# Group norm of the first and the last sequence by halves, with a logarithm and an exponential in PSUM; second weights held once; a new table of turns

## The chip, the cores and the metric

The kernel runs on one core of one Trainium2 chip. The metric is the device time of one execution in microseconds. Engines are named as in the profile: PE is the tensor engine (PEld its weight loads), DVE the vector engine, ACT the scalar engine, POOL the GpSimd engine, SP the engine that issues most DMAs.

## The reference

One RWKV block over 8 sequences of 256 tokens and 512 channels, float32, 32 heads of 16 channels. In short (E = 512, `_ln` is layer norm, `_token_shift` the row before minus this row):

```python
xn = _ln(x, ln1_w, ln1_b); sx = _token_shift(xn, state[:, i1])
xxx = tanh((xn + sx * maa_x) @ maa_w1)              # five groups of 32
x5 = xn + sx * (maa_stack + xxx @ maa_w2)           # five mixes
w = exp(-exp(time_decay + tanh(x5[1] @ decay_w1) @ decay_w2))
r, k, v, g = x5[3] @ Wr.T, x5[0] @ Wk.T, x5[2] @ Wv.T, silu(x5[4] @ Wg.T)
a = k * v;  out = r . (faaaa * a + s);  s = a + w * s   # per head, token by token
att = (a4 - mean) * rsqrt(var + 1e-5) * gn_w + gn_b     # group norm over 16 channels
x = x + (att * g) @ Wo.T
xn2 = _ln(x, ln2_w, ln2_b);  xk, xr = mixes of xn2 with the row before
x = x + sigmoid(xr @ ffn_Wr.T) * (relu(xk @ ffn_Wk.T) ** 2 @ ffn_Wv.T)
```

## The kernel before, in words

The work of each sequence b falls into three stages, each a function. `inputs_of_scan(b)` does the first layer norm, turns the rows so that channels lie on partitions (`psT1`), makes the five mixes (`psx`, `psm`, tiles `mix`, finished by POOL on L822 or L850), and projects r, k, v and g. The kernel's index q is a half of the 512 channels, m a quarter within it. `scan(b)` runs the recurrence in four blocks of channels. For each block four tiles `vs` are read back from DRAM, into which rows of v were stored (`vo`); DVE, or in a few places POOL (L998), multiplies them with k; DVE scans them along time (L1003); POOL multiplies the result with r (L1006, tiles `st`); and PE gathers the four products with narrow matmuls (L1014). `rest(b)` is group norm, the output projection (`pso`, L440 with Ws and g), the second layer norm, and the feed-forward part (`psfk`, `psfr`, `psfv`). The weights of the four large matrices of `rest` are streamed anew for every sequence.

Nothing is emitted as it is written. Every operation is recorded with its engine, an estimated duration, the buffers that it writes and reads, and for ACT the table and for PE the tile form that it wants. `Plan.order` then lays the operations out: each has a rank, a number from the table `TURNS`, and what is ready is taken by rank. The estimates (`LANDS` and `WAY` for transfers, others written at each operation) decide when a buffer is free and when something is ready, and the instructions of each engine are emitted in the order of their planned start. Each engine works in that order and waits for whatever is late. So a new table and new estimates move the instructions on all engines and both DMA queues.

PE's matmuls come in tile forms: full (128 rows by 128 columns), columns (four narrow matmuls of 32 output columns each), rows32 and rows64 (a part of the contraction rows), and turns through the identity. `Plan.tiles` decides where a projection is cut into narrow pieces, so as to change the form rarely.

Group norm in `rest(b)` before: the scan's output `att` is centred already. ACT squares both halves (L1032), PE averages the squares over each head's 16 channels with `C_MEAN` (L1040), each quarter of the channels onto 32 partitions of one tile `pv`. ACT takes the root (L1045), DVE the reciprocal (L1051). For sequences 0 to 6, ACT then spreads the 32 rows back over 128 partitions with 16 copies (L1073), and POOL multiplies `att` (L1076). For sequence 7, PE spreads them with `C_SEL` (L1059), and DVE multiplies (L1067). ACT applies gn_w and gn_b (L1080); POOL, or DVE for sequence 7, multiplies with g (L1085, L1083).

In `between`, which makes the feed-forward mixes of sequences 0 to 6, ACT writes two scaled copies, t and u, and POOL adds them (L736). The constants, the weights of the mixes (`w2a`, `w2b`) and of the decay (`dw2`) are loaded once at the start by SP's queue, with the large matrices; `w2b` holds the fifth mix's weights four times, once for each group of 32 rows, and `dw2` its weights twice.

## Time and profile before

| | us |
|---|---|
| median of 3 runs | 608.27 (606.26 to 608.39) |
| the profiled execution, first to last instruction | 607.4 |
| PE busy | 596.5 (98%) |
| DVE busy | 539.7 (89%) |
| ACT busy | 519.0 (85%) |
| POOL busy | 511.6 (84%) |

The profile is of one execution; its span, 607.4 us, is 0.9 us below the median of the runs. The record has no separate device time for the profiled execution, so the 0.9 us stand for what lies around the span. Busy times of different engines overlap. A busy PE is not PE at its peak, since the ends of its matmuls are modelled. In rows of groups, "x56" counts instructions, then come the busy time and the mean duration of one in nanoseconds, then the idle time ahead of them and what ended it. PE's rows count two records for each float32 matmul.

### The profile page before, as it was taken

How to read it: one execution, taken by the hardware profiler on the slowest of the kernel's cores; microseconds unless marked ns; L12 is line 12 of the kernel's file. 1: busy time of each engine (PE TensorE's matmuls, PEld its weight loads, DVE VectorE, ACT ScalarE, POOL GpSimd, SP SyncE). 2: the span in 40 equal slices, each digit the busy share in tenths (PEclk: the TensorE clock that was granted, in tenths of full speed). 3: DMA queues.
4: the chain of work that ended last, by engine and by line, in shares of the span. 5: the costliest groups of instructions: out<-in, count | busy, mean ns of one | idle time of the engine just before them, and what ended most of it. 6: DMA issues, size and time to landing. Idle time of an engine off the chain costs nothing.

```text
span 607.4 us, 17029 instructions
## 1 busy us (share of the span) xinstructions
PE 596.5 (98%) x7022; PEld 346.3 (57%) x7022; DVE 539.7 (89%) x492; ACT 519.0 (85%) x1177; POOL 511.6 (84%) x405
## 2 busy tenths in 40 slices
PE   9999998899999999999999999999999999999997
PEld 7575655347634774446654584465744474546464
DVE  5789999799999999998899999999899999995342
ACT  5977879979999999989999999999998899968350
POOL 2989999989979999899989899988889798987020
PEclk9999999799999999999999999999999999999999
DMA  9887695649668789669767987788667878972352
GB/s 316 272 198 209 184 253 170 167 119 284 193 162 227 198 250 244 182 191 253 202 196 214 269 215 213 210 256 216 166 184 195 231 202 216 282 206 74 130 187 77
DMA packets 52638, 124.73 MB, mean 205 GB/s; under 512 B 5841, under 2 KB 11345, under 8 KB 52561
## 3 DMA queue, kind: packets, MB, share of 16 engines
q1 hardware_dynamic: 48048, 119.39, 70.3%
q10 hardware_dynamic: 4512, 4.26, 2.2%
q8 instruction: 55, 0.90, 0.7%
q14 instruction: 23, 0.18, 0.1%
HBM read 115.25 MB, written 8.39 MB: 204 GB/s over the span
## 4 chain that ended last, share of the span: by engine, by line
PE 68%; POOL 14%; ACT 7%; DVE 5%; DMA 3%; issue 2%; SPq 0%; ACTq 0%; DVEq 0%; POOLq 0%
PE ps L440 57%; POOL st L1006 7%; PE ps L1014 7%; POOL mix L822 3%; PE ps L658 2%; POOL vs L998 1%; DVE st L1003 1%; DMA vo<-v 1%; PE ps L862 1%; PE ps L564 1%; DMA x<-in_x 1%; DMA vs<-vo 1%; DVE vs L1001 1%; ACT xh L595 1%; POOL mix L850 1%
## 5 line engine op out<-in xcount | busy, mean ns | idle before, releaser
L1003 DVE TENSOR_TENSOR_SCAN st<-wrep,vs 128x1024 f32<-128x1024 f32 x128 | 287.9, 2273 | 7.1 <-PE ps L1014 3.5
L1006 POOL TENSOR_TENSOR st<-st,r 128x1024 f32<-128x1024 f32 x128 | 254.8, 2008 | 7.4 <-DVE st L1003 6.0
L1001 DVE TENSOR_TENSOR vs<-vs,ps 128x1020 f32<-128x1020 f32 x122 | 142.6, 1199 | 2.0 <-ACT ps L980 1.0
L440 PE MATMUL ps<-Ws,mix 128*32 128x512 f32 (+3 forms) x872 | 115.1, 585 | 0.0
L440 PEld LDWEIGHTS ps<-Ws,mix 128*32 128x32 f32 (+1 forms) x872 | 37.5, 116 | 63.1 <-issue 58.5
L822 POOL TENSOR_TENSOR mix<-mix,xn 128x512 f32<-128x512 f32 x62 | 66.9, 1103 | 4.1 <-DVE mix L806 4.0
L1014 PE MATMUL ps<-st,con 128*32 128x256 f32 x1024 | 63.7, 388 | 2.4 <-POOL st L1006 1.6
L440 PE MATMUL ps<-mix,Wv 128*32 128x256 f32 (+1 forms) x832 | 59.5, 380 | 1.2 <-DVE mix L819 1.0
L440 PE MATMUL ps<-mix,Wk 128*32 128x256 f32 (+1 forms) x856 | 59.8, 380 | 0.0
L440 PE MATMUL ps<-mix,Wr 128*32 128x256 f32 (+1 forms) x712 | 59.2, 380 | 0.0
L440 PE MATMUL ps<-mix,Wg 128*32 128x256 f32 (+1 forms) x544 | 58.1, 380 | 0.1
L440 PE MATMUL ps<-Ws,g 128*32 128x512 f32 (+1 forms) x416 | 58.1, 606 | 0.0
L440 PE MATMUL ps<-mix,Ws 128*32 128x256 f32 (+1 forms) x688 | 57.8, 380 | 0.0
L1014 PEld LDWEIGHTS ps<-st,con 128*32 128x32 f32 x1024 | 33.1, 111 | 30.0 <-issue 9.0
L440 PEld LDWEIGHTS ps<-mix,Wg 128*32 128x32 f32 (+1 forms) x544 | 42.2, 133 | 12.8 <-issue 0.7
L440 PEld LDWEIGHTS ps<-mix,Wv 128*32 128x32 f32 (+1 forms) x832 | 36.6, 116 | 22.4 <-issue 3.0
L440 PEld LDWEIGHTS ps<-mix,Ws 128*32 128x32 f32 (+1 forms) x688 | 39.6, 123 | 16.7 <-issue 1.4
L440 PEld LDWEIGHTS ps<-mix,Wr 128*32 128x32 f32 (+1 forms) x712 | 38.8, 122 | 16.9 <-issue 1.3
L440 PEld LDWEIGHTS ps<-mix,Wk 128*32 128x32 f32 (+1 forms) x856 | 37.0, 115 | 19.8 <-issue 2.2
L804 ACT ACTIVATE ps<-ps,vec 128x256 f32<-128x256 f32 x112 | 45.5, 448 | 2.9 <-PE ps L440 2.0
L1170 ACT ACT_TABLE_LOAD x33 | 42.3, 1283 | 0.6
L736 POOL TENSOR_TENSOR mix<-mix,sx 128x512 f32<-128x512 f32 x28 | 35.5, 1279 | 6.6 <-ACT mix L729 3.7
(143 smaller groups left out, 1000.4 us busy)
## 6 DMA issues: line engine op xcount, KB each, us to landing
vs<-vo SPq DMA_DIRECT2D x128, 512.0 KB, 5.2
Ws<-in_wo SPq DMA_DIRECT2D x16, 512.0 KB, 5.4
Ws<-in_fk SPq DMA_DIRECT2D x16, 512.0 KB, 5.5
Ws<-in_fr SPq DMA_DIRECT2D x16, 512.0 KB, 5.7
Ws<-in_fv SPq DMA_DIRECT2D x16, 512.0 KB, 5.3
x<-in_x SPq DMA_DIRECT2D x9, 512.0 KB, 6.0
vo<-v ACTq DMA_DIRECT2D x15, 256.0 KB, 5.4
out<-o SPq DMA_DIRECT2D x15, 256.0 KB, 3.8
```

The lines of the kernel that those rows point to most:

```text
L440: nc.tensor.matmul(out[i : i + n], lhsT=w[:, i : i + n], rhs=x, start=first, stop=final)
L564: nc.tensor.matmul(ps()[:, 0, :], lhsT=warm[:, 0, 0:P], rhs=warm[:, 0, 0:T], start=True, stop=True)
L595: summed(junk[n], mv, [src[n]], lambda n=n: nc.scalar.activation(junk[n](), src[n](), AF.Copy, accum_out=mv()[:, n, 0:1]), 0)
L658: nc.tensor.transpose(to[:, m, n * P : (n + 1) * P], xh[n]()[:, k * P : (k + 1) * P], idt())
L736: gp(512, t, [t, u], lambda t=t, u=u: nc.gpsimd.tensor_tensor(t(), t(), u(), ALU.add))
L804: act(256, p_, [p_, vec], lambda g=g, q=q, m=m, p_=p_: nc.scalar.activation(p_()[:, m, :], p_()[:, m, :], AF.Identity, bias=col(f"maa_{g}" ...
L822: gp(512, t, [t, xn[q]], lambda q=q, t=t: nc.gpsimd.tensor_tensor(t(), t(), xn[q]()[:, :, 1 : T + 1], ALU.add))
L1001: dve(4 * T, [vs], [vs, kp], lambda m=m, vs=vs, kp=kp: nc.vector.tensor_tensor(vs()[:, :, 1:T], vs()[:, :, 1:T], kp()[:, m : m + 1, 1:T].t ...
L1003: dve(4 * T, [st], [w, vs, first], lambda w=w, vs=vs, st=st: nc.vector.tensor_tensor_scan(st().rearrange("p n t -> p (n t)"), w().rearrang ...
L1006: gp(4 * T, st, [st, r], lambda m=m, st=st, r=r: nc.gpsimd.tensor_tensor(st(), st(), r()[:, m : m + 1, :].to_broadcast([P, 4, T]), ALU.mul ...
L1014: nc.tensor.matmul(pat()[32 * i : 32 * i + 32, 0, :], lhsT=con()[:, s : s + 32], rhs=done[i]()[:, j, :], start=(j == 0), stop=(j == 3),)
L1170: nc.scalar.preload_act_table_set(op.table)
```

## The change

Four things are changed.

- Group norm of sequences 0 and 7. For each half q, eight narrow matmuls with `C_MEAN` put the mean square of every head onto all 128 partitions at once (a tile `pv` of 128 x 512 for each half). ACT takes the logarithm there and then exp(-0.5 x), both in PSUM and from one table, and DVE multiplies `att` with that tile. Root, reciprocal, the 16 copies, POOL's products of sequence 0 and PE's spreading of sequence 7 go. The planner lets an exponential run from the table of the logarithm.
- `w2b` and `dw2` are held once, cut by output channels, and `C_SEL` goes: 448 KB less are loaded at the start.
- The tiles `u` in `between` lie one element further into their buffer.
- The estimates for transfers are new, and so is the whole table `TURNS` (two of its lines stand for it).

```diff
-C_SEL = C_SUM + P
-NCONST = P + C_SEL + 2 * P
+NCONST = P + C_SUM + P
...
-    LANDS = {"vs__": (2.3, 2.45), "s": (0.3, 2.4), "vo_": (0.7, 2.2), "vo__": (0.35, 2.0), "o_": (0.7, 1.2), "x": (1.8, 2.3),
-             "xt": (1.7, 2.0), "xs": (0.7, 0.9), "idt": (0.2, 1.6), "Wfk_": (1.7, 2.7), "Wfr_": (1.7, 2.7),
-             "Wfv_": (1.7, 2.7), "Wo_": (1.7, 2.7)}
-    WAY = 1.4
+    LANDS = {"vs__": 2.33, "s": 0.4, "vo_": 0.85, "vo__": 0.25, "o_": 0.8, "x": 1.55, "xt": 1.5, "xs": 0.9, "idt": 0.2,
+             "Wfk_": 1.69, "Wfr_": 1.62, "Wfv_": 1.7, "Wo_": 1.7, "Wg": 1.6, "Wk": 1.2, "Wr": 1.1, "Wraw": 1.1, "cen": 0.4,
+             "con": 0.5, "dw": 0.5, "mw": 0.7, "mwa": 0.5, "mwb": 0.6, "vec": 0.6}
+    WAY, LANDED = 1.18, 1.15
     TABLES = {"exp": "exp_and_others", "tanh": "exp_and_others", "silu": "silu_and_others", "sig": "sigmoid_and_others",
-              "sqrt": "sqrt_and_others"}
+              "sqrt": "sqrt_and_others", "ln": "natural_log_exp_and_others"}
...
-            op.wire, op.lag = self.LANDS.get("".join(c for c in op.bufs[0].name if not c.isdigit()), (kb / 308, 1.7))
+            op.wire = self.LANDS.get("".join(c for c in op.bufs[0].name if not c.isdigit()), kb / 308)
+            op.lag = self.LANDED
...
     TURNS = """
-        8 72 12 20 41 124 40 135 48 116 79 78 141 119 3 32 84 31 128 181 183 185 11 10 19 39 62 68 36 65 69 37
...
+        2 122 24 50 18 104 49 77 105 42 54 133 87 85 1 29 31 26 142 159 160 163 19 17 43 22 47 51 20 46 68 21
...
                 elif now == "tanh" and want in ("exp", "silu"):
                     mode["ACT"] = now = want
+                elif want == "exp" and now == "ln":
+                    want = now
...
-            u = new("sx", f"u{name}_{q}")
+            u = Buf("sx", f"u{name}_{q}", lambda t: t[:, 1 : 2 * T + 1].rearrange("p (m t) -> p m t", m=2))
...
-                    mul(ps[k]()[:, 0, :], w2b()[rows, k * P : (k + 1) * P], tb()[rows, :], tiles=False)
+                    mul(ps[k]()[:, 0, :], w2b()[rows, :], tb()[rows, :], tiles=False)
...
-        pv, rs = new("ps", f"pv{b}"), sqs[0]
-
-        def mm():
-            for blk in range(NK):
-                rows = slice(32 * blk, 32 * blk + 32)
-                nc.tensor.matmul(
-                    pv()[rows, 0, :], lhsT=con()[:, C_MEAN : C_MEAN + 32], rhs=sqs[blk // 2]()[:, blk % 2 * T : blk % 2 * T + T],
-                    start=True, stop=True)
-
-        pe(0.437, [pv], [con, *sqs], mm, "columns")
-        act(256, rs, [pv, eh], lambda: nc.scalar.activation(
-            rs()[:, 0:T], pv()[:, 0, :], AF.Sqrt, bias=eh()[:, 0:1]), "sqrt", 1)
-        kept = False
-        if kept:
-            dve(256, [pv], [rs], lambda: nc.vector.reciprocal(pv()[:, 0, :], rs()[:, 0:T]), 6.25)
+        split = b == 0 or last
+        if split:
+            pr = []
+            for q, sq in enumerate(sqs):
+                p_ = new("ps", f"pv{b}_{q}")
+
+                def mm(sq=sq, p_=p_):
+                    for m in range(2):
+                        for i in range(0, P, 32):
+                            nc.tensor.matmul(p_()[i : i + 32, m, :], lhsT=con()[:, C_MEAN : C_MEAN + 32],
+                                             rhs=sq()[:, m * T : m * T + T], start=True, stop=True)
+
+                pe(0.864, [p_], [con, sq], mm, "columns")
+                act(512, p_, [p_, eh], lambda p_=p_: nc.scalar.activation(p_(), p_(), AF.Ln, bias=eh()[:, 0:1]), "ln", 1)
+                act(512, p_, [p_], lambda p_=p_: nc.scalar.activation(p_(), p_(), AF.Exp, scale=-0.5), "ln")
+                pr.append(p_)
         else:
+            pv, rs = new("ps", f"pv{b}"), sqs[0]
+
+            def mm():
+                for blk in range(NK):
+                    rows = slice(32 * blk, 32 * blk + 32)
+                    nc.tensor.matmul(
+                        pv()[rows, 0, :], lhsT=con()[:, C_MEAN : C_MEAN + 32], rhs=sqs[blk // 2]()[:, blk % 2 * T : blk % 2 * T + T],
+                        start=True, stop=True)
+
+            pe(0.437, [pv], [con, *sqs], mm, "columns")
+            act(256, rs, [pv, eh], lambda: nc.scalar.activation(
+                rs()[:, 0:T], pv()[:, 0, :], AF.Sqrt, bias=eh()[:, 0:1]), "sqrt", 1)
             dve(256, [rs], [rs], lambda: nc.vector.reciprocal(rs()[:, 0:T], rs()[:, 0:T]), 6.25)
-        if last:
-            pr = [new("ps", f"psr{b}_{q}") for q in range(NQ)]
-
-            def mm():
-                for m in range(2):
-                    for q in range(NQ):
-                        rows, s = slice(64 * q, 64 * q + 64), C_SEL + m * P
-                        nc.tensor.matmul(
-                            pr[q]()[:, m, :], lhsT=con()[rows, s : s + P], rhs=rs()[rows, 0:T], start=True, stop=True)
-
-            pe(0.945, pr, [con, rs], mm, "rows64")
         ys = []
         for q in range(NQ):
             att, g = got["att", q], got["g", q]
-            if last:
+            if split:
                 dve(512, [att], [pr[q], att], lambda att=att, ps=pr[q]: nc.vector.tensor_tensor(att(), ps(), att(), ALU.mult))
             else:
                 rsb = new("rk", f"rsb{b}_{q}") if q else sqs[1]
                 for n in range(2):
                     for i in range(4):
                         rows = slice(32 * i, 32 * i + 32)
-                        act(335 if kept else 376, rsb, [pv if kept else rs], lambda blk=2 * q + n, n=n, rows=rows, rsb=rsb: nc.scalar.copy(
-                            by_block(rsb)[rows, n, :],
-                            (pv()[:, 0, :] if kept else rs()[:, 0:T])[32 * blk : 32 * blk + 32, :]))
+                        act(376, rsb, [rs], lambda blk=2 * q + n, n=n, rows=rows, rsb=rsb: nc.scalar.copy(
+                            by_block(rsb)[rows, n, :], rs()[32 * blk : 32 * blk + 32, 0:T]))
...
-    load(con, consts[:, P:NCONST], 224)
+    load(con, consts[:, P:NCONST], 96)
     load(vec, vecs, 64)
     load(w1, maa_w1.rearrange("(k p) j -> p k j", p=P), 384)
-    load(w2a, maa_w2[0:4].rearrange("g j e -> (g j) e"), 256)
-    load(w2b, maa_w2[4:].rearrange("g j e -> (g j) e"), 256)
+    load(w2a, maa_w2, 256)
+    load(w2b, maa_w2_last, 64)
     load(dw1, decay_w1.rearrange("(k p) j -> p k j", p=P), 128)
-    load(dw2, decay_w2, 256)
+    load(dw2, decay_w2, 128)
...
-        "maa_w2": np.concatenate([a["maa_w2"], *[a["maa_w2"][4:]] * (3)], axis=0),
+        "maa_w2": a["maa_w2"][:4].reshape(4 * MAA, E),
+        "maa_w2_last": np.concatenate([a["maa_w2"][4][:, k * P : (k + 1) * P] for k in range(NK)], axis=0),
         "decay_w1": a["decay_w1"],
-        "decay_w2": np.concatenate([by_channel(a["decay_w2"].T).T] * 2, axis=0),
+        "decay_w2": np.concatenate(np.split(by_channel(a["decay_w2"].T).T, NQ, axis=1), axis=0),
```

How the new table moves instructions is shown at three places. The first is POOL ahead of the gather of sequence 1's first block. Rows with 128x1024 are the products of scanned tiles with r (L1006 before, L1011 now), `mix` rows finish mixes of sequence 2, and `vs` is the product of a tile with k. Before:

```order
L822 TENSOR_TENSOR mix_119<-mix_119,xn_101 128x512
L822 TENSOR_TENSOR mix_122<-mix_122,xn_102 128x512
L822 TENSOR_TENSOR mix_115<-mix_115,xn_102 128x512
L822 TENSOR_TENSOR mix_111<-mix_111,xn_101 128x512
L998 TENSOR_TENSOR vs_149<-vs_149,k_127 128x4x255
L1006 TENSOR_TENSOR st_156<-st_156,r_128 128x1024
L1006 TENSOR_TENSOR st_159<-st_159,r_128 128x1024
L1076 TENSOR_TENSOR att_141<-att_141,sq_162 128x2x256
L1076 TENSOR_TENSOR att_142<-att_142,rk_153 128x2x256
L1006 TENSOR_TENSOR st_155<-st_155,r_128 128x1024
L1085 TENSOR_TENSOR g_138<-att_141,g_138 128x512
L1085 TENSOR_TENSOR g_137<-att_142,g_137 128x512
```

And now, on the same engine (L827 is L822 of before, L1003 is L998, L1091 is L1085):

```order
L1003 TENSOR_TENSOR vs_149<-vs_149,k_127 128x4x255
L827 TENSOR_TENSOR mix_115<-mix_115,xn_101 128x512
L1011 TENSOR_TENSOR st_156<-st_156,r_128 128x1024
L827 TENSOR_TENSOR mix_122<-mix_122,xn_101 128x512
L827 TENSOR_TENSOR mix_111<-mix_111,xn_102 128x512
L1011 TENSOR_TENSOR st_155<-st_155,r_128 128x1024
L1011 TENSOR_TENSOR st_157<-st_157,r_128 128x1024
L1091 TENSOR_TENSOR g_137<-att_141,g_137 128x512
L1091 TENSOR_TENSOR g_138<-att_142,g_138 128x512
```

The two group norm products are gone, and the product with k stands ahead of three mixes that it followed before.

The second place is PE at the same gather: two pieces of a k projection, the fifth mix of sequence 2 (`tb`, `mw2b`), and the gather's first row, before:

```order
L440 MATMUL ps_175<-mix_122,Wk_76 32x256 x8
L440 MATMUL ps_175<-mix_111,Wk_77 32x256 x8
L440 MATMUL ps_175<-tb_124,mw2b 128x256
L440 MATMUL ps_172<-tb_124,mw2b 128x256
L440 MATMUL ps_174<-tb_124,mw2b 128x256
L440 MATMUL ps_177<-tb_124,mw2b 128x256
L1014 MATMUL ps_175<-st_155,con 32x256
```

Now the gather follows the k projection at once; this is PE from the gather's last row on (L445 is L440 of before, L1019 is L1014), with the output projection of sequence 0 (`Ws`, `g`):

```order
L1019 MATMUL ps_172<-st_155,con 32x256
L445 MATMUL ps_175<-Ws_168,g_137 32x512 x8
L445 MATMUL ps_175<-Ws_169,g_138 32x512 x8
L445 MATMUL ps_173<-Ws_168,g_137 32x512 x8
L445 MATMUL ps_172<-tb_124,mw2b 128x256
L445 MATMUL ps_177<-tb_124,mw2b 128x256
L445 MATMUL ps_175<-tb_124,mw2b 128x256
L445 MATMUL ps_174<-tb_124,mw2b 128x256
L445 MATMUL ps_173<-Ws_169,g_138 32x512 x8
```

The fifth mix moved from ahead of the gather to between the output projections.

The third place is the start of SP's queue. `Ws` are the raw weights of v (two halves) and a small matrix from `consts`, `mw` the first mixing weights, `dw` the first decay weights. Before:

```order
L429 DMA xt_88<-in_x 128x512 x2
L429 DMA Ws_167<-in_wv 128x2x512
L429 DMA Ws_168<-in_consts 128x128
L429 DMA vec<-in_vecs 128x128
L429 DMA Ws_169<-in_wv 128x2x512
L429 DMA mw_66<-in_maa_w 128x4x192
```

Now:

```order
L434 DMA xt_88<-in_x 128x512 x2
L434 DMA Ws_167<-in_wv 128x2x512
L434 DMA mw2a<-in_maa_w 128x512
L434 DMA Ws_168<-in_consts 128x128
L434 DMA vec<-in_vecs 128x128
L434 DMA Wk_77<-in_wk 128x2x512
L434 DMA Ws_169<-in_wv 128x2x512
L434 DMA dw_69<-in_decay_w 128x4x64
L434 DMA mw_66<-in_maa_w 128x4x192
```

Three loads (256, 512 and 128 KB) moved ahead of the first mixing weights. Counted over the whole order, PE changes its tile form 97 times now and 101 times before; ACT has 36 loads of tables now and 34 before; PE has 24 more narrow matmuls for group norm and 4 fewer wide ones for spreading.

More of the change, by code (lines that the diff above doesn't have):

```diff
@@ L364, in tables @@
                 want = "silu" if want == "silu" else "exp"
+            elif want == "exp" and mode == "ln":
+                want = mode
             if want != mode:
@@ L388, in tile_rwkv_block @@
     maa_w2: bass.AP,
+    maa_w2_last: bass.AP,
     decay_w1: bass.AP,
@@ L421, in tile_rwkv_block @@
         "x2": lambda t: t[:, :, 1 : E + 1],
+        "sx": lambda t: t[:, 0 : 2 * T].rearrange("p (m t) -> p m t", m=2),
     }
@@ L452, in tile_rwkv_block @@
     idt, con, vec = const("idt", [P, P]), const("con", [P, NCONST - P]), const("vec", [P, NK, NVEC + 2 * NB])
-    w1, w2a, w2b = const("mw1", [P, NK, 6 * MAA]), const("mw2a", [P, E]), const("mw2b", [P, E])
-    dw1, dw2 = const("dw1", [P, NK, DEC]), const("dw2", [2 * DEC, E])
+    w1, w2a, w2b = const("mw1", [P, NK, 6 * MAA]), const("mw2a", [P, E]), const("mw2b", [P, P])
+    dw1, dw2 = const("dw1", [P, NK, DEC]), const("dw2", [2 * DEC, 2 * P])
     hm = const("hm", [P, NK, 32])
@@ L470, in tile_rwkv_block @@
     pool("xn", 4, [P, 2, T + 1])
-    pool("sx", 4, [P, 2, T])
+    pool("sx", 4, [P, 2 * T + 2])
     pool("mix", 14, [P, 2, T])
@@ L885, in mm @@
                 for q in range(NQ):
-                    rows, k = slice(DEC * q, DEC * q + DEC), 2 * q + m
-                    mul(pw[q]()[:, m, :], dw2()[rows, k * P : (k + 1) * P], hd()[rows, 1, :], tiles=False)
+                    rows = slice(DEC * q, DEC * q + DEC)
+                    mul(pw[q]()[:, m, :], dw2()[rows, m * P : (m + 1) * P], hd()[rows, 1, :], tiles=False)
         pe(0.945, pw, [dw2, hd], mm, "rows64", ws)
@@ L1182, in _constants @@
             con[:, C_SUM + 32 * i + 4 * h + i] = head == h
-            con[32 * i + 4 * h, C_SEL + P * (i % 2) : C_SEL + P * (i % 2 + 1)] = head_v == h
     same = head_v[:, None] == head_v[None, :]
```

267 rows, old and new, of the table TURNS are left out of this document.

## The prediction

> **What bounds the kernel now.** I read the page's sums first, then the busy time by stage, the waits of the tensor engine, and the chain that ended last.
>
> ```profile
> span 607.4 us, 17029 instructions
> PE 596.5 (98%) x7022; PEld 346.3 (57%) x7022; DVE 539.7 (89%) x492; ACT 519.0 (85%) x1177; POOL 511.6 (84%) x405
> ```
>
> PE is the bound over the whole span. The stages say where it is not. The columns are span, then busy time of PE, PEld, DVE, ACT and POOL with counts, the granted clock, the DMA share and GB/s.
>
> ```profile
> 0.00:15.00 15.00, 13.78 (x86) 11.76 (x90) 8.44 (x24) 8.19 (x19) 4.02 (x20) 1.00 0.92 315
> 45.00:105.00 60.00, 57.94 (x1020) 34.52 (x1016) 60.00 (x52) 49.26 (x103) 60.00 (x43) 1.00 0.77 209
> 105.00:120.00 15.00, 12.23 (x190) 6.51 (x184) 10.81 (x11) 14.21 (x33) 15.00 (x10) 0.85 0.58 147
> 120.00:135.00 15.00, 15.00 (x184) 6.12 (x180) 13.74 (x11) 12.24 (x29) 12.73 (x12) 0.93 0.51 132
> 135.00:555.00 420.00, 419.86 (x4990) 240.87 (x4979) 405.38 (x332) 390.46 (x900) 386.28 (x294) 1.00 0.77 214
> ```
>
> From 135 to 555 us PE is busy 419.86 of 420: there only fewer matmuls or fewer changes of form shorten anything. Up to 120 us POOL and DVE are full (60.00 of 60 each), PE has idle time, and right after it the clock falls. A finer cut of the same view:
>
> ```profile
> 95.40:98.80 3.40, 2.37 (x46) 1.30 (x41) 3.40 (x5) 3.32 (x7) 3.40 (x4) 1.00 0.87 211
> ...
> 112.00:115.40 3.40, 1.49 (x24) 0.52 (x16) 2.73 (x2) 3.35 (x8) 3.40 (x4) 1.00 0.91 234
> 115.40:118.80 3.40, 2.54 (x24) 1.18 (x28) 1.40 (x4) 3.37 (x10) 3.40 (x4) 0.50 1.01 240
> 118.80:122.20 3.40, 3.40 (x24) 0.99 (x20) 2.23 (x2) 3.30 (x7) 3.40 (x3) 0.50 0.91 228
> ```
>
> In 112.0 to 115.4 PE was busy 1.49 of 3.40 us, and then ran at half clock for 6.8 us, which is 3.4 us of full-speed work lost. With 2.37 of 3.40, in 95.4 to 98.8, nothing followed. PE's waits in the span, longest in total first:
>
> ```profile
> PE ps L1014 <- POOL st L1006: 1.6, 1, 1.6
> PE ps L440 <- ACT k L901: 1.2, 1, 1.2
> PE ps L862 <- POOL mix L822: 1.0, 1, 1.0
> ```
>
> The chain that ended last (start, us, what) names what holds that place up:
>
> ```profile
> 38.70 2.37 POOL vs L998
> ...
> 108.18 3.98 POOL st L1006 x2
> 112.16 2.09 POOL att L1076 x2
> 114.25 1.97 POOL st L1006
> 116.26 3.64 PE ps L1014 x32
> 119.90 10.89 PE ps L440 x104
> 130.78 1.86 PE ps L1014 x32
> ...
> 174.71 1.73 PE ps L1014 x32
> ...
> 381.55 0.48 PE ps L1040 x8
> ...
> 559.81 3.43 PE ps L440 x32
> 563.24 1.06 PE ps L1059 x8
> ```
>
> POOL's window between the first of these rows and the gather at 116.26 is a block without a hole, and two products of `rest(0)` follow it:
>
> ```profile
> 38.70:116.20 77.50, 77.50 (x53) 0.99 0.74 197
> 116.14 2.16 POOL L1085 TENSOR_TENSOR g<-att,g 128x512 f32<-128x512 f32 x2
> ```
>
> So the gather of sequence 1's first block (L1014) stands at 116.26 because POOL has 77.5 us of work in a row ahead of it, and 2.09 of them are the two group norm products L1076 of sequence 0, which the change takes off POOL.
>
> **The change part by part.** Prices, by groups (busy, mean ns of one, idle before):
>
> ```profile
> L1073 ACT COPY rk<-sq 32x256 f32<-32x256 f32 x56 | 22.5, 402 | 1.3 <-ACT v L901 0.4
> L1051 DVE RECIPROCAL sq<-sq 128x256 f32<-128x256 f32 x8 | 13.9, 1736 | 2.5 <-ACT sq L1045 2.5
> L1067 DVE TENSOR_TENSOR att<-ps,att 128x512 f32<-128x512 f32 x2 | 1.3, 685 | 1.9 <-PE ps L1059 1.9
> L1100 ACT ACTIVATE mix<-ps 128x512 f32<-128x512 f32 x16 | 9.3, 588 | 7.2 <-PE ps L440 7.2
> L1080 ACT ACTIVATE att<-att,vec 128x256 f32<-128x256 f32 x32 | 17.3, 592 | 3.5 <-DVE att L1067 3.3 <-POOL att L1076 0.2
> L1170 ACT ACT_TABLE_LOAD x33 | 42.3, 1283 | 0.6
> L736 POOL TENSOR_TENSOR mix<-mix,sx 128x512 f32<-128x512 f32 x28 | 35.5, 1279 | 6.6 <-ACT mix L729 3.7 <-ACT sx L734 2.8
> L822 POOL TENSOR_TENSOR mix<-mix,xn 128x512 f32<-128x512 f32 x62 | 66.9, 1103 | 4.1 <-DVE mix L806 4.0
> L440 PE MATMUL ps<-tb,mw2b 32*128 32x256 f32 x64 | 5.7, 426 | 1.2 <-ACT k L901 1.2
> ```
>
> *Norm of sequence 0, engine by engine.* ACT loses 16 copies (16 x 0.402 = 6.4 us) and a root, and gains four 512-wide passes over PSUM. No row has a logarithm; the nearest, L1100, is as wide and reads PSUM too, so 4 x 0.59 = 2.4, and 4.7 if it takes twice as long; either is less than what goes. DVE loses a reciprocal (1.74) and gains two products (2 x 0.69). POOL loses 2.09. PE now has 16 narrow matmuls for the norm, 32 records, for which the chain has 1.73 (L1014 x32), where it had 8 records, 0.48: +1.25. All but POOL's part lies beside POOL's full block; on the path stands -2.1.
>
> *What this moves at the gather.* With POOL still full from 38.70, the last product of that block is done at 116.2 - 2.1 = 114.1, and the two L1085 products end at 116.3. The output projection of sequence 0 (L440, Ws and g) waits for both; before, it started at 119.90, since the gather in front of it ran at half clock (3.64 against 1.73). Gain: 119.9 - 116.3 = 3.6. Is PE there in time? POOL's order now has the long L998 product ahead of the last three mixes and only two block products behind them, so the last mix comes at 114.1 - 3.98 = 110.1. The k projection that needs it (two groups of 32 records, 3.5) ends at 113.6, half a microsecond before the gather can start. PE's idle time is then spread in pieces of about 1, 0.5 and 0.5 us ahead of the r projection, the k projection and the gather, instead of 1.2 and 1.6 within one 3.4 us window, and the 1.25 us of new matmuls lie in it.
>
> *The clock.* If no 3.4 us window falls below half, 2.3 us at half clock after 119.9 go too: -1.15. [...]
>
> *Moved matmul.* The last mix of sequence 2 (tb, mw2b) leaves the place before the gather, where it filled a wait, and now stands between the output projections: 5.7 / 8 = +0.7 on the path.
>
> *Norm of sequence 7.* PE: 1.73 against 0.48 + 1.06 = 1.54 (L1040 and L1059, whose spreading matmul goes), so +0.2 on a PE that is full. The chain of the second half is two passes (2 x 0.59), three other ACT passes queued behind them (3 x 0.59, DVE's product of 0.69 beside them), four L1080 (4 x 0.59) and a product (0.69): 6.0 us. Its cover is the receptance projection, whose four halves are twice the 3.43 row, 6.9 us. So it is hidden with 0.9 to spare; if that cover is gone, the output projection of sequence 7 waits for the excess alone.
>
> *Tables.* Two loads more, 36 against 34: 2 x 1.28 = 2.6 us of an ACT that is busy 390 of 420 and waits elsewhere; 0 on the path. [...]
>
> *Offset of the `u` tiles.* POOL's sum of two tiles at an equal offset takes 1279 ns, with one moved by an element 1103: 28 x 0.18 = 4.9 us less on POOL, all after 135 us where PE is full: 0.
>
> *Loads.* 448 KB less, and a new order: the rows on the first mixing weights (mw) are
>
> ```profile
> 3.56 0.47 SPq L429 DMA_DIRECT2D mw<-in_maa_w  x1
> mw<-in_maa_w SPq DMA_DIRECT2D x1, 384.0 KB, 6.4
> 11.20 1.96 PE L440 MATMUL ps<-mix,mw 128*128 128x256 f32 x8
> ```
>
> They land at 10.0 and are used at 11.2. Now 896 KB more go first (mw2a, half of Wk, dw1); at 315 GB/s 2.9 us, so they land at 12.9 and the first mixing starts 1.7 us late. All loads end 448 KB / 315 = 1.4 us sooner, and the first stored rows of v queue behind the loads. What counts is POOL's start at 38.70, which hangs on those DMAs: between -1.4 and +1.7; I take +0.2, nearer the middle since both act.
>
> *New turns elsewhere.* PE changes its tile form 97 times instead of 101. A gather with a change takes 1.86, without 1.73: 4 x 0.13 = -0.5. The bounds are 0 and a new wait, which the rivals hold.
>
> *Sum:* -3.6 - 1.15 + 0.7 + 0.2 + 0.2 - 0.5 = -4.1 us. The profiled span goes from 607.4 to 603.3. The runs have a median of 608.27, 0.9 above the span, so the time becomes 604.2 us.
>
> **The rivals.**
> 1. *The clock still halves.* POOL still ends PE's waits, so idle time stays before the gather. It decides if PE is busy for less than some share of a 3.4 us window, which lies between 1.49 and 2.37 us by the two rows above. For it: my pieces of 0.5, 0.5 and the wait for L1085 fall close together. Against: 1.0 alone did not bring it. Price +3.4: 607.6 us.
> 2. *The late start goes through.* POOL starts 1.7 instead of 0.2 late because the mixing weights are late: +1.5, 605.7 us; and with more of PE idle in front, the clock may fall as well: 609.1.
> 3. *Slower: DVE waits for the logarithm.* DVE works in order and is full (60.00 of 60). Its new product of `att` with PSUM waits, if they are not done, for PE's group, a table load and two passes (0.87 + 1.28 + 1.18 = 3.3 us), with scans queued behind it, and each late scan is a late POOL. At one half this is 3.3, at both 6.7; from 4.1 on the gain is gone, PE waits before the gather again and the clock falls as now: 608.3 - 4.1 + 6.7 + 3.4 = 614.3 us. Against: ACT has 10.7 us of idle time in 45 to 105, and the products stand several scans behind their groups.
> 4. *All waits vanish.* 1.6 + 1.2 + 1.0 and 3.4 of clock: 608.3 - 7.2 = 601.1.
>
> **How the numbers follow.** The forecast has 0.54, rival 1 0.20, rival 2 0.10, rival 3 0.11, rival 4 0.05. The forecast's own range is 602.5 to 605.7. For 8 in 10 I reach to 600.8 on one side (rival 4) and to 609.2 on the other (rivals 1 and 2, leaving rival 3 out). A measurement tells apart about 0.5%, 3.0 us: faster means under 605.2. The forecast lies there but for a small part, and rival 4: 0.54 for faster. Rivals 1 and 2 and the rest of the forecast are within: 0.34. Slower: rival 3 and a clock that falls twice, 0.12.
>
> **What would show it.** Right: no L1076 products for sequence 0; the gather after them starts at about 114 and the output projection at about 116.3; granted clock 1.00 in 105 to 135; loads of tables 2 more; L736's heir at about 1.1 us; POOL still full from about 39 to 116. Wrong: a half-clock stretch anywhere past 20 us (rival 1); POOL's first L998 after 40 (rival 2); DVE idle ahead of the new product with a wait on ACT (rival 3); a PE wait on ACT or DVE near 565 (cover of sequence 7 gone).

## The result, and the profile after

The changed kernel takes 609.8 us (median of 12 runs in two sets of six; 607.84 to 611.37), the kernel before 607.0 and 606.5 beside the two sets, and 606.2 to 607.0 beside all the runs below. The ratio is 1.0052 with an interval of 1.0029 to 1.0075 in the first set and 1.0052 (1.0032 to 1.0071) in the second: half a per cent slower, where 604.2 us, 0.7% under its base of 608.3, was forecast. Three of the 110 executions of the kernel before that ran beside the experiments took 691, 1040 and 2196 us, and the ratios leave them out.

The page of the changed kernel, the lines that answer to those of before:

```profile
span 606.1 us, 17579 instructions
PE 595.6 (98%) x7302; PEld 341.6 (56%) x7302; DVE 541.0 (89%) x492; ACT 520.2 (86%) x1169; POOL 504.9 (83%) x403
```

Its busy time by stage (span, then PE, PEld, DVE, ACT, POOL with counts, granted clock, DMA share, GB/s):

```profile
0.00:15.00 15.00, 12.30 (x74) 10.20 (x78) 7.60 (x20) 7.50 (x15) 3.04 (x17) 1.00 0.90 319
...
105.00:120.00 15.00, 14.93 (x246) 7.67 (x239) 14.31 (x10) 12.72 (x28) 15.00 (x12) 1.00 0.64 163
120.00:135.00 15.00, 14.58 (x190) 7.88 (x183) 14.73 (x16) 13.24 (x34) 13.69 (x11) 1.00 0.91 252
135.00:555.00 420.00, 418.91 (x5127) 236.03 (x5129) 402.71 (x329) 391.81 (x897) 379.86 (x293) 1.00 0.76 208
```

At the gather everything stands where it was forecast: PE is busy 14.93 of 15 between 105 and 120, the clock is 1.00 throughout, and POOL's block begins at 39.15 and ends with the two products at 116.65, which is 114.54 + 2.11 (forecast: 116.3), as the chain says:

```profile
39.15 2.36 POOL vs L1003
...
110.58 3.96 POOL st L1011 x2
114.54 2.11 POOL g L1091 x2
```

But PE starts worse (12.30 of the first 15 us, before 13.78) and is no longer full from 135 to 555 (418.91, before 419.86). The prices of the groups came out as forecast: the logarithm 0.66 us, the exponential 0.58, POOL's sum of two tiles 1.09, and two loads of tables more:

```profile
L1053 ACT ACTIVATE ps<-ps,eh 128x512 f32<-128x512 f32 x4 | 2.6, 662 | 0.2 <-PE ps L1049 0.2
L1054 ACT ACTIVATE ps<-ps 128x512 f32<-128x512 f32 x4 | 2.3, 582 | 0.1
L741 POOL TENSOR_TENSOR mix<-mix,sx 128x512 f32<-128x512 f32 x28 | 30.3, 1091 | 5.0 <-ACT mix L734 4.8 <-ACT xn L673 0.2
L1176 ACT ACT_TABLE_LOAD x35 | 44.9, 1283 | 0.6
```

In all six runs of the first set, time less span is 1.7 to 1.8 us, and the spans go from 606.1 to 609.4. The forecast had taken 0.9 us for time less span, from the kernel before, so the first run below is of that kernel.

### The profile page after: what moved, and what is told of

It is laid out like the page before. It is cut to its first block, busy times and chain, and to the rows that moved or that the text cites. A ratio compares the mean times of both kernels' runs of the same rounds, so it can differ in the third digit from the quotient of the medians.

```text
span 606.1 us, 17579 instructions
## 1 busy us (share of the span) xinstructions
PE 595.6 (98%) x7302; PEld 341.6 (56%) x7302; DVE 541.0 (89%) x492; ACT 520.2 (86%) x1169; POOL 504.9 (83%) x403
## 4 chain that ended last, share of the span: by engine, by line
PE 61%; POOL 13%; DVE 9%; DMA 7%; ACT 6%; issue 3%; SPq 0%; ACTq 0%; DVEq 0%
PE ps L445 51%; PE ps L1019 6%; POOL st L1011 6%; DVE st L1008 4%; DMA vs<-vo 3%; POOL mix L827 3%; PE ps L663 2%; POOL vs L1003 2%; DVE vs L1006 1%; DMA vo<-v 1%; PE ps L867 1%; DMA x<-in_x 1%; DVE mix L811 1%; ACT att L968 1%; DMA mw2a<-in_maa_w 1%
## 5 line engine op out<-in xcount | busy, mean ns | idle before, releaser
L1011 POOL TENSOR_TENSOR st<-st,r 128x1024 f32<-128x1024 f32 x128 | 254.6, 2002 | 13.8 <-DVE st L1008 12.9
L1006 DVE TENSOR_TENSOR vs<-vs,ps 128x1020 f32<-128x1020 f32 x122 | 142.6, 1200 | 0.7 <-ACT ps L985 0.6
L445 PE MATMUL ps<-Ws,mix 128*32 128x512 f32 (+3 forms) x920 | 115.1, 586 | 0.1
L445 PEld LDWEIGHTS ps<-Ws,mix 128*32 128x32 f32 (+1 forms) x920 | 36.6, 115 | 64.0 <-issue 57.4
L827 POOL TENSOR_TENSOR mix<-mix,xn 128x512 f32<-128x512 f32 x62 | 66.7, 1092 | 6.5 <-DVE mix L811 5.6
L1019 PE MATMUL ps<-st,con 128*32 128x256 f32 x1024 | 62.9, 381 | 1.1 <-ACT g L936 0.9
L445 PE MATMUL ps<-mix,Wv 128*32 128x256 f32 (+1 forms) x856 | 60.2, 380 | 0.3 <-DVE mix L824 0.3
L445 PE MATMUL ps<-mix,Wr 128*32 128x256 f32 (+1 forms) x688 | 59.8, 380 | 0.0
L445 PE MATMUL ps<-mix,Wk 128*32 128x256 f32 (+1 forms) x880 | 59.3, 379 | 0.0
L445 PE MATMUL ps<-mix,Ws 128*32 128x256 f32 (+1 forms) x760 | 57.9, 379 | 0.7 <-DVE mix L716 0.7
L445 PE MATMUL ps<-mix,Wg 128*32 128x256 f32 (+1 forms) x592 | 58.2, 380 | 0.0
L445 PE MATMUL ps<-Ws,g 128*32 128x512 f32 (+1 forms) x464 | 57.4, 593 | 0.0
L445 PEld LDWEIGHTS ps<-mix,Wg 128*32 128x32 f32 (+1 forms) x592 | 42.1, 129 | 13.4 <-issue 1.0
L445 PEld LDWEIGHTS ps<-mix,Ws 128*32 128x32 f32 (+1 forms) x760 | 38.3, 119 | 19.5 <-issue 2.6
L445 PEld LDWEIGHTS ps<-mix,Wv 128*32 128x32 f32 (+1 forms) x856 | 36.8, 115 | 21.5 <-issue 2.0
L445 PEld LDWEIGHTS ps<-mix,Wr 128*32 128x32 f32 (+1 forms) x688 | 39.4, 123 | 16.3 <-issue 1.3
L1019 PEld LDWEIGHTS ps<-st,con 128*32 128x32 f32 x1024 | 32.5, 110 | 28.0 <-issue 7.1
L445 PEld LDWEIGHTS ps<-mix,Wk 128*32 128x32 f32 (+1 forms) x880 | 36.7, 114 | 20.5 <-issue 1.8
L999 ACT ACTIVATE vs<-s,cm 128x4 f32<-128x4 f32 x128 | 35.6, 296 | 5.5 <-DMA vs<-vo 4.6
```

Of the source, the lines that this page charges most:

```text
L445: nc.tensor.matmul(out[i : i + n], lhsT=w[:, i : i + n], rhs=x, start=first, stop=final)
L827: gp(512, t, [t, xn[q]], lambda q=q, t=t: nc.gpsimd.tensor_tensor(t(), t(), xn[q]()[:, :, 1 : T + 1], ALU.add))
L999: plan.add("ACT", 0.19336, [first], [s0, cm, landed], lambda i=i, blk=blk, vs=vs: nc.scalar.activation(vs()[:, :, 0:1], s0()[:, blk, 4 * i ...
L1006: dve(4 * T, [vs], [vs, kp], lambda m=m, vs=vs, kp=kp: nc.vector.tensor_tensor(vs()[:, :, 1:T], vs()[:, :, 1:T], kp()[:, m : m + 1, 1:T].t ...
L1011: gp(4 * T, st, [st, r], lambda m=m, st=st, r=r: nc.gpsimd.tensor_tensor(st(), st(), r()[:, m : m + 1, :].to_broadcast([P, 4, T]), ALU.mul ...
L1019: nc.tensor.matmul(pat()[32 * i : 32 * i + 32, 0, :], lhsT=con()[:, s : s + 32], rhs=done[i]()[:, j, :], start=(j == 0), stop=(j == 3),)
```

## The experiments

Two terms return below: e5 is the change without its new order, and "lost time" is the time that passed less the matmuls' own length. For that length one full matmul of 256 columns, or four narrow ones side by side, counts the same in every row: 1.2% less than 0.432 us, the most frequent distance of two such matmuls in the traces of the kernel before and of the changed one. The choice moves the levels and hardly the differences: counted with 0.432 us, the first profiles of these two have 6.6 us less each by 600 us, and still lie 3.2 apart. Medians of the kernel before differ by up to 0.8 us between sets of runs, so a difference of that size between two sets shows little by itself.

**The base, and the parts of the change one by one (e1 to e4).**

e1, the kernel before, unchanged.

> The kernel before, unchanged, to see each run's span beside its time. Time less span: about 0.9 us in every run, as in the one profile of before (608.3 less 607.4), where the changed kernel has 1.77 in all six. Theory L (landings: the new turns leave less room for DMAs to land late): the spans lie within 605.3 to 607.5, closer together than the 606.1 to 609.4 of the changed kernel, and what spread there is goes with the granted clock. Rival O (the new order is simply longer, whatever the DMAs do): says nothing else here.

606.76 us. Time less span is 1.7 to 1.8 us in each of its 12 runs, so what lies around the span did not change, and the execution profiled at first, with its span of 607.4, took about 609.2 us: 2 to 3 us more than the usual run. The spans go from 602.9 to 606.2. In 7 of the 12 runs the mean granted clock is 0.996 or 0.997; in the other 5 it is 1.000 and four of those are the four shortest. The first profile had 0.994. Theory L's range is missed (the spans spread by 3.3 us, as the first six of the changed kernel do), but part of the spread does go with the clock. The profile of e1 fell on the shortest run. Its view of the cores, then its chain of waits:

```profile
core 0: 602.9 us, clock 1.000
```

```profile
37.16 2.34 POOL vs L998
...
114.68 1.93 PE ps L1014 x32
116.61 9.66 PE ps L440 x104
```

This is the kernel before, with nothing changed, and its output projection (L440) starts at 116.61, not at 119.90: 3.3 of the 3.6 us that the forecast put down to the removed products lie between two executions of the same kernel. POOL's block starts 1.5 us sooner here. The profile names ACT and DVE as what PE waits for ahead of the gather, and no POOL product (PE's waits of e1, longest first, then the last step of the chain):

```profile
PE ps L1014 <- DVE cm L941: 1.5, 1, 1.5
PE ps L440 <- ACT k L901: 1.3, 1, 1.3
```

```profile
114.53 0.14 DVE cm L941
114.67 0.01 issue
114.68 1.93 PE ps L1014 x32
```

POOL's last product ahead of the gather (L1006) ends at 114.61 in the same trace, 0.06 us before DVE. So two paths of about the same length end here, and a shorter one through POOL need not bring the gather forward.

e2, the changed kernel, unchanged.

> The changed kernel, unchanged, for a second profile. Time less span 1.77 again. Spans again 606 to 609.5 at a clock of 1.00. Theory L: a profile of a longer run differs from the first (606.1) by a few stalls of one to two us at places where a loaded vs tile is awaited, past 135 us, with the same busy time of PE. Rival O: a longer run has its extra time spread evenly, in no single wait, or in busy time of PE.

609.78 us, spans 606.1 to 609.6, time less span 1.7 to 1.8. The second profile has a span of 608.2. From 135 to 555 PE is busy 1.1 us less than in the first:

```profile
135.00:555.00 420.00, 417.79 (x5089) 235.43 (x5091) 403.40 (x330) 390.14 (x896) 377.54 (x291) 1.00 0.76 208
```

The largest of its waits in total is on ACT for `ta` (2.0 us in three waits); e10 takes up the longest, of 1.1. The lost time between the two profiles is in pieces of 0.2 to 1 us in many places: that decides for neither theory.

e3, before with the second weights held once:

```diff
-const("mw2b", [P, E])                      load(w2b, maa_w2[4:]..., 256)
+const("mw2b", [P, P])                      load(w2b, maa_w2_last, 64)
-const("dw2", [2 * DEC, E])                 load(dw2, decay_w2, 256)
+const("dw2", [2 * DEC, 2 * P])             load(dw2, decay_w2, 128)
```

> Before with the second weights held once (mw2b 64 KB from an input of its own, dw2 128 KB) and nothing else; 320 KB less to load. Theory W (the additional input tensor makes the time around the span): time less span 1.7. Rival N (the norm, with its table set and its 280 more matmuls, makes it): 0.9. Span: the loads end 320 KB / 315 GB/s = 1.0 us sooner, so POOL's block starts up to 1.0 earlier: span 0 to 1.0 us under that of the kernel before; 0 if POOL's start hangs on something else.

606.88 us, 1.0010 of before (0.9996 to 1.0024), time less span 1.7 to 1.8: no effect of the weights is to be seen, and POOL's block starts at 37.1, where e1 has 37.2. Both theories on the time around the span fall: there was nothing to explain.

e4, before with the new norm. The diff is that of the change's `rest`; in the table of turns only the 32 entries of the norm's own operations are new.

> Before with the new norm of sequences 0 and 7 alone: old weights, old offset of u, old turns and cost tables, with new places only for the norm's own instructions. Theory N: time less span 1.7; theory W: 0.9. Span, theory L and my prediction's steps: the two POOL products go (-2.1), the clock no longer halves (-3.4 and -1.15), two groups more of PE stand in front of the gather (+1.25): 603 to 605 against 606 to 607.4. Rival O (the norm's work on PE eats the gain): 606.5 to 608.

605.72 us, 0.9994 (0.9982 to 1.0007). Spans 603.4 to 605.9, and the clock fell in 1 run of 12 instead of 7. Where it didn't fall the median span is 603.9, against 603.6 in the five such runs of e1: at full clock the norm gains nothing, and what it brings is a clock that falls less often (here and in e5 in 5 of 24 runs; in the kernel before beside all the runs in 63 of 107). The spans lie where theory L had them, but the 3 us between them and the usual run of before are not there: the medians are 603.9 and 605.0.

**All but the order (e5).** The changed kernel's code, with the cost tables and the turns of before:

```diff
-    LANDS = {"vs__": 2.33, "s": 0.4, ...}      WAY, LANDED = 1.18, 1.15
+    LANDS = {"vs__": (2.3, 2.45), ...}         WAY = 1.4
-    TURNS (new)
+    TURNS (before, with the norm's entries of e4)
```

> The changed kernel's computation, weights, tables and offset of u, but with the turns and the cost tables of before (the norm's own instructions placed as in e4). Theory T (the loss is in the new turns): 605.7 us, as e4 without the new weights and offset. Rival U (the new weights or the offset of u cost something): 607 or more.

605.39 us, 0.9996 (0.9980 to 1.0011). Theory T holds: norm, weights and offset together are not slower than before, and the new order, turns and cost tables together, costs 4.4 us. The clock fell in 4 of the 12 runs. This run also shows what the two products were worth at the gather in the old order (e5's chain):

```profile
115.38 0.14 DVE cm L944
115.52 0.01 issue
115.53 1.93 PE ps L1017 x32
```

The products are gone, POOL's last product ahead of the gather ends at 114.24, and the gather still starts at 115.53, later than in e1, because DVE is what PE waits for. DVE now makes the two products itself (0.68 and 0.69 us), and waits 0.6 us for ACT's exponential ahead of the second. In e4's profile it is the same: POOL ends at 115.01, the gather starts at 115.98, on DVE.

**Cutting the order in two (e6 to e8, e9, e11).** Each operation got its turn of before or its new turn, by the time at which its order starts it.

> The changed kernel with the turns of before for all work that the old order starts before 45 us (the loads among it), the new turns after that. The lost time of PE in the profiles (time less the matmuls' own length) says that the new order loses 1.3 us more than before up to 30 us, 0 to 0.6 from there to 90, wins 2.1 between 90 and 120, and loses again 0.8 from 120 to 150, 0.2 to 1.0 to 180, 1.1 to 1.5 from 360 to 390, and about 1 at the end. Theory P (the loss is these pieces, each from its own place in the order): 609.8 less 1.3 to 2: 607.8 to 608.5. Rival D (delays of landing DMAs anywhere, which an earlier start doesn't mend): 609.5.

609.7 us, 1.0074 (1.0045 to 1.0103), rival D's number, and the clock fell in 3 of the 6 runs. The 1.3 us at the start are saved in the profile (lost time 7.35 by 30 us), but behind the cut PE waits for `g`, which the new order needs sooner than the old one makes it, so the run decides nothing.

```profile
PE ps L859 <- ACT g L928: 2.3, 1, 2.3
```

> As e6, with the turns of before for all work up to 140 us and the new turns after. Theory P: the start's 1.3 to 2 and the 0.8 after the gather are saved, the gain of 2.1 at the gather is given up: 609 to 610. If the new turns after 140 us cost nothing: 605.7.

611.33 us, 1.0088 (1.0062 to 1.0114).

> As e6, with the turns of before for all work up to 345 us and the new turns after. Theory P: what stays is the piece from 360 to 390 and the end, 2 to 2.5 us over e5: about 608. If the late part of the new order costs nothing: 605.7; a time above e7's: the cut itself disturbs.

610.1 us, 1.0071 (1.0050 to 1.0092). Both were slower than their theories had it; the clock fell in 4 of 6 runs of e7 and in 1 of 6 of e8. Ahead of these cuts the old order, under the new cost tables, lost 1.5 and 2.5 us more by 135 than in e5, in profiles where the clock fell after the gather. So the sums can't be read; the part behind the cut can, in e8: 11.4 us lost from 345 to 600, 8.25 in e5. Theory P's times fall in all three runs; its late part is borne out by that loss alone.

> The reverse of e8: the changed kernel with the new turns up to 345 us and the turns of before after that. Theory L (most of the loss is late in the order: 345 to 390 us and the end; PE loses 11.4 us in e8 from 345 to 600 and 8.25 in e5): 609.8 less 2.5 to 3.2: 606.6 to 607.3, with spans as close together as those of e5. Rival S (the loss lies at the start and around the gather, and e8 was slow by its cut alone): 609 to 610.

607.79 us, 1.0014 (1.0001 to 1.0027), 2.0 less than the changed kernel, and the 12 spans lie within 605.5 and 606.9. Nearly half of the loss is behind 345 us, and so is much of the spread. Theory L holds in its direction; the gain is less than its 2.5 to 3.2.

> As e6 with the cut at 80 us, where the two orders have done nearly the same work, so that the cut disturbs less: old turns for the loads and all work up to 80, new ones after. Theory: PE's lost time by 75 us 8.9 and not 10.5 to 11.2, POOL's block starts at 37.2 to 38.7, the gather stays at about 113 to 115 at full clock: 1.3 to 1.6 under the changed kernel, 608.2 to 608.5. Rival (what is won at the start is taken back by POOL's block, which then waits elsewhere): 609.8.

607.33 us, 1.0005 (0.9989 to 1.0021): 2.5 less, more than expected. Cut at a place where both orders have done the same work, the start is a part of the loss as large as the late one; the intervals of e9 and e11 overlap, so which is larger is not decided.

Lost time of PE up to a time, worked out from the matmuls of each profile (us; the first row is the execution profiled at first; the span of each stands ahead; the first profile of the changed kernel is its shortest run, e2's is near its median of 608.0, and e11's is the longest of its 12, which have a median of 605.6):

```
                 span     30     75    105    135    345    405    570    600
before          607.4   7.35   9.45  13.42  20.16  27.15  29.57  35.07  36.03
before, e1      602.9   7.35   8.81  11.71  15.88  22.87  25.34  30.37  32.19
all but order, e5 603.3 7.35   8.86  12.14  15.45  22.23  24.61  29.09  30.48
changed         606.1   8.63  10.51  13.74  15.66  22.87  26.31  31.12  32.83
changed, e2     608.2   8.63  11.15  14.16  16.30  24.38  28.23  32.93  34.75
old turns <80, e11 608.4 7.56  9.23  12.67  14.81  22.02  26.53  33.36  35.18
e12             602.6   7.35   8.97  12.14  14.38  21.59  24.06  28.67  30.48
```

**What in the late part (e10).** In both profiles of the changed kernel PE waits for `ta` at about 373 us, for 0.7 and 1.1 us. SP's timeline in the first, and the `vs` load among the DMA issues of that stretch (KB each, us from issue to landing):

```profile
360.72 0.37 SPq L434 DMA_DIRECT2D xt<-in_x  x1
361.18 0.42 SPq L434 DMA_DIRECT2D Ws<-in_fr  x1
362.10 0.52 SPq L434 DMA_DIRECT2D vs<-vo  x1
362.71 0.54 SPq L434 DMA_DIRECT2D Ws<-in_fv  x1
```

```profile
vs<-vo SPq DMA_DIRECT2D x1, 512.0 KB, 8.6
```

The chain goes from that load to ACT's sequencer, which has a store of v's rows next in its queue (L981), then over `ta` to PE:

```profile
359.87 2.21 DVE st L1008
...
362.10 7.64 DMA vs<-vo
...
370.79 0.37 ACTq L981
...
372.69 0.28 ACT ta L786
```

```profile
ACT ps L848 <- issue: 1.7, 1, 1.7
```

The `vs` load is issued when its buffer comes free (DVE's row ends at 362.08); in the order of before (e5) `xt` and both weights come behind it, and now 1 MB goes ahead of it. e10 puts these two loads behind it again:

```diff
 SP's queue at 361 us
-xt  Wfr3_1  vs5_1_0  Wfv3_0  s
+vs5_1_0  xt  Wfr3_1  Wfv3_0  s
```

> The changed kernel with two places changed in the queue of loads: at about 361 us the load of xt for sequence 7 and the second load of Wfr of sequence 3 go behind the vs load that is issued 1 us later and landed 8.6 us after its issue, where 4.3 to 6 are usual. Theory B (that vs load is late because 1 MB goes ahead of it, ACT waits for it with its work on ta queued behind, and PE for ta): the vs load lands in 5 to 6 us, ACT's wait at 370 and PE's wait for ta of 0.7 to 1.1 go, PE's lost time from 360 to 375 falls from 1.75 to 0.7: 1.0 us under the changed kernel, 608.8. Rival (the load is late for its buffer, which comes free at 362.1 in either order): no difference.

608.35 us, 1.0025 (1.0010 to 1.0040), 1.4 less than the changed kernel. The load now lands in 5.6 us, and ACT's wait is gone:

```profile
vs<-vo SPq DMA_DIRECT2D x1, 512.0 KB, 5.6
```

```profile
ACT ps L847 <- issue: 0.2, 1, 0.2
```

(L847 is L848 of the changed kernel.) PE's lost time from 360 to 375 is 1.11 and not 1.75 (2.18 in e2). Theory B holds; the 1.4 us are more than the 0.6 to 1.1 that this stretch lost less.

**What at the start (e13 to e15).** The chain of the changed kernel into POOL's block:

```profile
25.34 8.92 DMA vo<-v
34.26 0.02 issue
34.27 4.80 DMA vs<-vo
39.08 0.07 issue
39.15 2.36 POOL vs L1003
```

The second store of v's rows (`vo<-v`) takes 8.9 us, behind four `vs` loads. In e1 three go ahead of it (DMA issues of that stretch):

```profile
vs<-vo SPq DMA_DIRECT2D x3, 512.0 KB, 7.1
vo<-v ACTq DMA_DIRECT2D x1, 128.0 KB, 6.7
```

e13 moves the fourth behind the first load of the second half, and with it the scan work on that tile on ACT, DVE and POOL:

```diff
 SP's queue from 23 us on
-vs0_0_2  vs0_0_3  vs0_0_1  vs0_0_0  vs0_1_3  vs0_1_0
+vs0_0_2  vs0_0_3  vs0_0_1  vs0_1_3  vs0_0_0  vs0_1_0
```

> The changed kernel with one load moved at the start: the fourth vs load (the last of the first half of sequence 0) goes behind the second store of v's rows and the first vs load of the second half, as before; the scan work on that tile goes a few places later on ACT, DVE and POOL. Theory F (four loads of 512 KB ahead of the second store of v's rows, where before had three, make POOL's block start late): that store lands at 32.5 to 33.5 and not at 34.3 to 35.3, POOL's block starts at 37.2 to 38.2 and not at 38.6 to 39.7, the time falls by 512 KB / 315 GB/s = 1.7: 608.2. Rival W (what counts is the late landing of mw and PE's late first mixing, 1.3 us, which this doesn't mend): no change, 609.8.

608.75 us (7 runs), 1.0033 (1.0017 to 1.0050): 1.0 of the 1.7 expected, in an interval that overlaps that of the changed kernel. The store takes 7.8 us and lands at 33.4, as theory F has it, and POOL starts without a wait for a DMA, but at 38.8:

```profile
L1003 POOL TENSOR_TENSOR vs<-vs,k x1: 2347/2347/2347, 38.8 to 38.8; 128x1020 f32<-128x1020 f32 x1
```

So the store came as expected and POOL's start did not: 38.8 lies outside theory F's 37.2 to 38.2, and e10, which leaves this load where it was, has 38.6.

> e13 and e10 together: three loads moved in the queue of the changed kernel, nothing else. If both are causes of their own: 609.8 less 1.5 (e10) and 1.7: 606.6, so that two places in SP's queue make up most of the 4.4 us between the changed kernel and e5. If e10's gain was by chance: 608.

607.43 us, 1.0018 (1.0006 to 1.0031). The two gains add (1.4 and 1.0 from 609.8 make 607.4): three loads, moved by one or two places in the queue, and the scan work that goes with one of them, are 2.4 of the 4.4 us. Against e10 alone the fourth load is worth 0.9 here, so its gain was seen twice. How it comes about is not shown: POOL's block starts at 39.2 in this profile, and PE's lost time by 105 us is 13.4 in e13 and 13.8 here, against 13.7 and 14.2 in the changed kernel and 13.4 in e10.

> e14 and one change more in the queue of loads at the start: mw, the first mixing weights, goes ahead of mw2a, half of Wk and dw1 (896 KB), as before. Theory M (my rival 2: the late mixing weights delay all that follows, POOL's block too, and are the second half of the start's loss): mw lands at 9.6 to 10.0 and not at 11.5 to 11.7, PE has lost 7.4 us by 30 us and not 8.6 to 9.2, POOL's block starts at 37.2 to 38 and not at 39.2, the time falls by 1.2: 606.2. Rival (PE's own new order at the start is what is long, whenever mw lands): 607.4, as e14.

608.29 us, 1.0028 (1.0011 to 1.0044): no gain. `mw` landed at 9.57, but the clock fell in 8 of 12 runs, in the profile right at the start (the same columns as above):

```profile
13.10:16.50 3.40, 1.61 (x21) 1.11 (x20) 1.83 (x6) 0.96 (x4) 0.17 (x1) 1.00 1.06 396
16.50:19.90 3.40, 2.96 (x14) 2.03 (x15) 2.08 (x5) 3.40 (x8) 3.04 (x5) 0.50 1.07 399
```

In the 4 runs at full clock the span is 605.7 to 606.0, where e14 has a median of 605.7: there too nothing is gained, and theory M's 1.2 us fall. Its other signs can't be read, since this profile ran at half clock from 16.5 us to 23.3. So moving these weights ahead does not bring back the rest of the start's loss; which part of the new order there makes it stays open.

**The best of both (e12).** Old turns up to 80 us and from 200 on, the new ones between, around the gather:

> A version meant to beat both: the changed kernel's computation, with the turns of before up to 80 us and from 200 us on, and the new turns only between, around the gather. e5 less the 2.1 that PE loses less between 105 and 120, plus 0.75 (120 to 135) and 0.3: 604.4, clock 1.00 in all runs. Rival (the cuts cost what the piece wins): 605.5 to 607.

604.38 us (604.31 to 604.85; 6 runs), 0.9955 of before (0.9938 to 0.9972), 0.5% faster: the expected number. The clock is 1.000 in all six runs and the spans agree within 0.6 us. Its page, and the two stages that count:

```profile
span 602.6 us, 17297 instructions
```

```profile
105.00:120.00 15.00, 14.85 (x227) 9.09 (x216) 14.69 (x11) 12.27 (x27) 15.00 (x11) 1.00 0.69 185
...
135.00:555.00 420.00, 419.77 (x5022) 239.91 (x5024) 401.56 (x330) 389.89 (x895) 380.14 (x294) 1.00 0.76 209
```

## Why the prediction was wrong, point by point

- **The base failed.** "The runs have a median of 608.27, 0.9 above the span": the profiled execution was not one of these runs. Time less span is 1.7 to 1.8 us in every run, not 0.9, so it took about 609.2, 2 to 3 us above the medians since (606.2 to 607.0), with POOL's start 1.5 us late and 6.8 us at half clock (115.4 to 122.2; mean clock 0.994, which 1 run of 12 in e3 and none in e1 had). Three runs of before, at 608.39, 608.27 and 606.26, showed the spread; the sum took one execution for the kernel.
- **The gather: the place came true, the gain did not.** The step that failed is "on the path stands -2.1", and with it the "Gain: 119.9 - 116.3 = 3.6". In the changed kernel the output projection starts at 116.34, as forecast, but in e1 the kernel before starts it at 116.61, and in e5, without the two products, the gather waits for DVE until 115.53. So POOL was not alone in holding the gather; a path through ACT and DVE was as long. The -3.6 and the -1.15 of clock were differences to one execution. That the place came out right is in part luck: it was reckoned from a POOL start of 38.70, later than the usual 37.2, and the new order starts POOL at 39.15. Against the same code in the old order (e12 and e5) the new order there brings 1.0 us, 0.8 where the clock did not fall.
- **The clock: right in where it would not fall, not shown in its condition.** That it falls when PE is busy for less than half of 3.4 us, or, as rival 1 had it, for less than some share between 1.49 and 2.37 us, is not shown: from 112.0 to 115.4 PE was busy 1.49 us in the first profile of before, which then ran at half clock, and 1.44 in e1, which did not. With the new order at the gather PE was busy 3.33 of the 3.40 us from 112.9 to 116.3, in the first profile of the changed kernel. The clock fell in 7 of 12 runs of before (e1), in 5 of 24 with the new norm in the old order (e4, e5), and in 1 of 73 with the new order at the gather (the changed kernel and e9 to e14; e6 and e15 made gaps elsewhere). But four in ten runs of before did not fall and had nothing to gain here.
- **"+0.2 (POOL start)" failed:** the old order up to 80 us takes 2.5 us off (e11). Two effects were set against each other, sooner end of the loads and later `mw`. `mw` did land late, at 11.5 and not at 9.6 as in e1 (12.9 was forecast), and POOL's block starts 2.0 us later than in e1; but `mw` moved ahead on top of e14 brings nothing (e15), and about 1.0 comes with one `vs` load that stood ahead of a store (e13, e14). Rival 2 had the sign and a price of 1.5, but the run on its cause found no gain.
- **"-0.5 (new turns elsewhere)" failed:** +2.0 behind 345 us (e9), 1.4 of it from two loads put ahead of a `vs` load that ACT waits for (e10). The bound "0 and a new wait" had been left to rivals that all stood before 135 us or took waits away; none looked at SP's queue past 135 us, where PE was full in the row and so seemed safe.
- **What is not placed.** Start 2.5, late part 2.0, gather -1.0: 3.5 of the 4.4 us, each uncertain by about 1 us by the scatter of the runs, and the cuts have costs of their own. No run tested the stretch from 135 to 345 us alone; in the table PE loses 1.3 us more there in e2 than in e5 (0.4 in the first profile of the changed kernel).
- **Costed at nothing or little, and not contradicted:** the weights (e3); the norm on PE (e4, no more than 0.3 us at full clock); the offset and the loads of tables, which were tested only together, in e5. PE has no wait longer than 0.4 us between 555 and 580, so sequence 7's norm is hidden as worked out. Rival 1 did not come (clock 0.999 or 1.000 in 11 of 12 runs), nor did rivals 3 (in e4 and e5 its wait is 0.6 us) and 4.

## What to carry to other kernels

One profile is one execution: put its own time beside the runs before summing gains against it, and see in a second profile of the same kernel whether the wait that is to go is there, and what else ends at the same moment. Where an order changes, read the DMA queue as closely as the engines': here 1 MB of loads put ahead of one whose buffer had just come free delayed it by 3 us (8.6 against 5.6 in e10), ACT waited 1.7 us behind it, and PE, which had been full, 0.7 us for ACT. An order is not good or bad as a whole; cut it where both orders have done the same work, and keep the pieces that win.

## What the runs showed of the hardware that was not expected

- The clock falls, in the same kernel, in some executions only: in 63 of the 107 executions of before, and in 7 of the 12 of e1. In e1's run at full clock PE was busy 0.74 of the 3.40 us ahead of the gather, and 1.44 from 112.0 to 115.4, both less than the 1.49 of the first profile, and nothing followed:

```profile
111.30:114.70 3.40, 0.74 (x12) 0.35 (x13) 2.89 (x4) 3.37 (x9) 3.40 (x4) 1.00 1.00 247
114.70:118.10 3.40, 3.40 (x48) 1.68 (x52) 2.26 (x3) 3.35 (x9) 3.40 (x3) 1.00 1.05 246
```

```profile
112.00:115.40 3.40, 1.44 (x24) 0.83 (x28) 2.19 (x3) 3.37 (x9) 3.40 (x3) 1.00 1.01 231
```

  In the profiles where it fell, PE was busy 1.49 of the 3.40 us ahead of the fall in the first profile (half clock from 115.4 us), 1.57 in e7 (from 115.4), 1.43 in e8 (from 116.9) and 1.61 in e15 (from 16.5). The first profile and e15 then stood at 0.50 for 6.8 us, with a mean clock of 0.994; e7 and e8 have 0.50 in the 3.40 us after it began, and a mean clock of 0.997. So PE's busy time in the 3.40 us ahead, as these traces give it, does not tell the executions with a fall (1.43 to 1.61) from the one without (0.74 and 1.44); what decides it stays open.
- The same 512 KB load lands 8.6 us after its issue with 1 MB issued in the 1.4 us ahead of it, and 5.6 us without (e10): here the order in which the loads were issued changed how long this one took to land.
